# The residual and second bias of a graph network's node update: rows of x added by DVE, in place of a PE product of x's columns

## The chip, the cores and the metric

The kernel runs on one core of one Trainium2 chip. The metric is the device time of one execution in microseconds (us). The engines are named as in the profile: PE multiplies matrices (PEld loads its weights), DVE works on vectors, ACT applies activations, POOL issues the gathers, SP issues plain transfers; ACT issues some too.

## The reference

A graph with 12,500 nodes of 64 features and 200,000 edges sorted by destination. For every edge a two-layer network computes a message; messages are summed per destination; a second two-layer network updates the node, and the node's own row is added and normalised:

```
msg_in     = concatenate([nodes[row], nodes[col], edge_features])   # 64 + 64 + 32
messages   = relu(msg_in @ mW1 + mb1) @ mW2 + mb2                   # 160 -> 128 -> 64
aggregated = segment_sum(messages, col, num_segments=12500)
upd        = relu(concatenate([nodes, aggregated]) @ uW1 + ub1) @ uW2 + ub2
out        = layernorm(x + upd)                                      # over 64 features, no scale
```

## The kernel before

**The first layer by tables.** The products of all nodes with the two node parts of mW1 are made once, as tables in device memory: A (tab_a) for sources and B (tab_b) for destinations, the latter with the bias added. The products need x by columns. In `columns_of` (L396 to L402) all of x's columns are loaded into one large tile, `xall`, by eight transfers at the very start: four on SP's queue for the lower 64 partitions and four on ACT's for the upper. `products` multiplies eight blocks of 128 nodes per call, `chunk_a` (13 chunks) copies one half with ACT and the other with DVE and stores on ACT's queue; `chunk_b` adds the bias on DVE and stores on SP's queue. All of A and the first chunk of B are made before the main loop; the other twelve chunks of B in the loop, from step 8 on.

**Steps.** An edge tile is 128 edges. A step is eight tiles (SUB); there are 196 steps. For step s, POOL gathers the source rows with eight indirect transfers (`gather`, L168). As A is not there at the beginning, the first XG = 7 steps gather rows of x instead (64 features), which PE transposes and multiplies with w1a (`transpose`, and the branch `s < XG` of `node_part`). Two such steps share one of the 14 row buffers; later steps have one buffer each, and `frees(s)` says after which step a buffer can be gathered into again. `windows` issues, on SP, eight transfers of 32 rows of B (L229), since a tile's destinations lie within a window of 32 nodes; `load` and `loadd` (L215, L184) load the edges' features and destinations for two steps at a time, the former after DVE's `select` (L194 to L200) has compared destinations. `edge_part` (L255) multiplies these on PE; `node_part` adds the gathered rows on DVE (L276) and ACT takes the relu (L277); `collect` (L302) sums the hidden rows of a window on PE with a selection matrix, and L307 counts the edges.

**Updates.** The second message layer is folded into the update's weights (`weights`). A period of steps collects up to 448 nodes; there are 34 periods, which start at the steps in `UPD`. At a period's end `close` copies sums and counts, `carry` moves an overlap of 32 nodes on, and `update` (L337, L338) makes the hidden layer. One step later `residual` makes four blocks of 128 nodes: per block one product of x's columns (tile `xw`: row 0 the counts, row 63 ones, below them 64 rows of x) with `ux`, which holds a unit matrix and, in row 63, the second bias (L346), and one of the hidden layer with `u2` (L347). Both accumulate in PSUM tile `py`, which shares two buffers (tag "pc") with the edge products. DVE takes mean and variance from `py` (L351, L353), ACT a square root (L355). A step later `norm` normalises from `py` (L361, L364), and `store` writes on SP's queue (L370). `columns`, two steps ahead of the update, loads `xw` (L330).

**Order.** Every engine's order of work is the program's, written out by hand (`manual_schedule`); waits come from the tiles' uses. In a step of the main loop it is: gathers whose buffers are due, `norm`, `windows(s+2)`, `node_part(s)`, `collect(s-1)`, `close`, then `select`, `load` and `counts` (even steps) or `loadd` (odd), a chunk of B, `edge_part(s+1)`, `carry`, `update`, `residual`, `columns`, the set-up in `rest`, `store`. The pool `work` has two buffers per name.

A general path (`tc.If`, for inputs whose destinations don't fit the windows) does not run with these inputs.

Of the kernel before, what the change touches and what calls it, by code (L numbers as in the profile page):

```python
# [10 lines left out]
F32 = mybir.dt.float32  # L11
I32 = mybir.dt.int32
AF = mybir.ActivationFunctionType
ALU = mybir.AluOpType
# [3 lines left out]
P = 128  # L18
N, D, DE, DH = 12500, 64, 32, 128
E = 200000  # L20
EPS = 1e-5
NB = -(-N // P)
# [12 lines left out]
PADWIN = 1000000  # L35
EK, SK = 0, DE
ROWB = 14
XG = 7
NCH = 8
HB = NCH // 2  # L40
EARLY = NCH * P
# [3 lines left out]
NCOL = (-(-N // P) + UB) * P  # L45
UN = 448
UW = UN + WIN
ONE = D - 1


def updates():
# [12 lines left out]


@with_exitstack
def gnn_kernel(ctx: ExitStack, tc: tile.TileContext, x1T, x, eT, e_rows, src, dst, dst_row, wrow, wnext, whalf,
               mW1, mb1, mW2, mb2, uW1, ub1, uW2, ub2, out):


# [36 lines left out]
    xall = const.tile([P, -(-NB // NCH), HB * P], F32, name="xall")  # L107
    w1b = const.tile([P, DH], F32, name="w1b")
    b1 = const.tile([P, DH], F32, name="b1")

# [12 lines left out]
    ux = const.tile([P, D], F32, name="ux")  # L123
# [49 lines left out]
    with tc.tile_pool(name="sup", bufs=2) as sup, tc.tile_pool(name="work", bufs=2) as work, tc.manual_schedule():  # L173
# [152 lines left out]
        def columns(u):  # L326

            n0 = nc.values_load(usup[0:1, u:u + 1], engines=[ET.SP], min_val=0, max_val=N - 1,
                                skip_runtime_bounds_check_because="destinations are node numbers")
            nc.sync.dma_start(xw[u % 2][ONE:, :UN], x1T[:, bass.ds(n0, UN)])  # L330
            us[u] = n0

        def update(u):

            n0 = us[u]
            pu = psum.tile([DH, UN], F32, name="pu", tag="pc")
            nc.tensor.matmul(pu, w2u, sums_s[u % 2][:, :UN], start=True, stop=False)  # L337
            nc.tensor.matmul(pu, uz, xw[u % 2][:, :UN], start=False, stop=True)  # L338
            nc.scalar.activation(hT[:, :UN], pu, AF.Relu, bias=ub1_s)

        def residual(u):

            n0 = us[u]
            py = psum.tile([P, UB, D], F32, name="py", tag="pc")
            for i in range(UB):
                nc.tensor.matmul(py[:, i], xw[u % 2][:, i * P:(i + 1) * P], ux, start=True, stop=False)  # L346
                nc.tensor.matmul(py[:, i], hT[:, i * P:(i + 1) * P], u2, start=False, stop=True)  # L347
            st = work.tile([P, UB, nc.vector.BN_STATS_DIM], F32, name="st")
            mv = work.tile([P, UB, nc.vector.BN_AGGR_DIM], F32, name="mv")
            for i in range(UB):  # L350
                nc.vector.bn_stats(out=st[:, i], in_=py[:, i])  # L351
            for i in range(UB):
                nc.vector.bn_aggr(out=mv[:, i], in_=st[:, i])  # L353
            sd = work.tile([P, UB], F32, name="sd")
            nc.scalar.activation(sd, mv[:, :, 1], AF.Sqrt, bias=eps)  # L355
            us[u] = (n0, py, mv, sd)

        def norm(u):
            n0, py, mv, sd = us[u]
            rs = work.tile([P, UB], F32, name="rs")  # L360
            nc.vector.reciprocal(rs, sd)  # L361
            o = work.tile([P, UB, D], F32, name="o")
            for i in range(UB):
                nc.vector.tensor_scalar(o[:, i], py[:, i], mv[:, i, 0:1], rs[:, i:i + 1],  # L364
                                        op0=ALU.subtract, op1=ALU.mult)
            us[u] = (n0, o)

# [18 lines left out]


        Av, Bv, B0v = (t.rearrange("(c p) f -> p c f", p=P) for t in (A, B, B0))
        xblocks = x1T[1:, :].rearrange("d (c n) -> d c n", n=P)

        def spread(c):

            n = min(NCH, NB - c)
            return [(h, min(HB, n - HB * h)) for h in range(2) if n > HB * h]

        def columns_of(h, a, b, queue):  # L396

            b = min(b, -(-(NB - HB * h) // NCH))
            if b > a:
                v = xblocks[:, a * NCH + HB * h:, :]  # L400
                queue.dma_start(xall[64 * h:64 * h + 64, a:b].rearrange("d c (i n) -> d c i n", n=P),
                                bass.AP(v.tensor, v.offset, [[v.ap[0][0], D], [NCH * P, b - a], [P, HB], [1, P]]))  # L402

        def products(c, w):
            xl = xall[:, c // NCH]
            pb = psum.tile([P, 2, HB, DH], F32, name="pb", tag="pc")
            for i in range(HB):
                for h, m in spread(c):
                    if i < m:
                        nc.tensor.matmul(pb[:, h, i, :], xl[64 * h:64 * h + 64, i * P:(i + 1) * P],  # L410
                                         w[64 * h:64 * h + 64], start=True, stop=True)
            return pb, work.tile([P, 2, HB, DH], F32, name="tb")

        def chunk_a(c):
            pb, tb = products(c, w1a)
            for h, m in spread(c):
                if h:
                    nc.vector.tensor_copy(tb[:, h, :m], pb[:, h, :m])  # L418
                else:
                    nc.scalar.copy(tb[:, h, :m], pb[:, h, :m])  # L420
            n = min(NCH, NB - c)
            nc.scalar.dma_start(Av[:, c:c + n, :], tb.rearrange("p h i f -> p (h i) f")[:, :n])

        def chunk_b(c, into):
            pb, tb = products(c, w1b)
            n = min(NCH, NB - c)
            pf, tf = (t.rearrange("p h i f -> p (h i) f")[:, :n] for t in (pb, tb))
            nc.vector.tensor_tensor(tf, pf, b1.unsqueeze(1).broadcast_to([P, n, DH]), op=ALU.add)
            for v in into:
                nc.sync.dma_start(v[:, c:c + n, :], tf)  # L430
# [24 lines left out]
        nc.scalar.dma_start(src_s[:, :64], src[:, :64])  # L455
        for h in range(2):
            nc.sync.dma_start(w1a[64 * h:64 * h + D], mW1[0:D, :])
        for a, b in ((0, 1), (1, 3), (3, 7), (7, 13)):
            columns_of(0, a, b, nc.sync)
            columns_of(1, a, b, nc.scalar)  # L460
        nc.scalar.dma_start(src_s[:, 64:], src[:, 64:])
        make_identity(nc, ident)
        nc.gpsimd.iota(slot_i, pattern=[[1, WIN]], base=0, channel_multiplier=0)
# [20 lines left out]
        for k, c in enumerate(range(0, NB, NCH)):  # L484
            chunk_a(c)
            if k == 0:
                chunk_b(0, [B0v, Bv])
            if k == 2:

                w0 = wint[:, :GE * SUP]  # L490
                nc.vector.tensor_scalar(past, w0[:, GE * SUP - 1:], float(EARLY - WIN), None, op0=ALU.is_gt)
                nc.vector.tensor_scalar(w0, w0, float(EARLY - WIN), None, op0=ALU.min)
                windows(0)
                windows(1)
            if k == 4:
                relative(0, 8 * SUP)
            if k == 6:
                offsets()
            if k == 9:
                select(0)  # L500
                load(0)
                counts(0)

        def rest(s):

            if s == 1:
                relative(8 * SUP, 8 * SUP + WCH)
            elif s == 2:
                relative(8 * SUP + WCH, NT)
                halves(4 * SUP, NTP // 2)  # L510
            elif s == BS:
                nc.sync.dma_start(wa, wrow.rearrange("o (p c) -> (o p) c", c=SUP))
                nc.sync.dma_start(wb, wnext.rearrange("o (p c) -> (o p) c", c=SUP))
                nc.scalar.dma_start(w2, mW2)
                nc.scalar.dma_start(u1a, uW1[D:2 * D, :])
                nc.scalar.dma_start(b2c, mb2.rearrange("(f o) -> f o", o=1))
                nc.vector.memset(uz[:D], 0.0)
                nc.vector.memset(ux[:D], 0.0)
                nc.vector.memset(eps, EPS)
# [63 lines left out]
        for s in range(last + 3):  # L583
# [203 lines left out]
```

## Time and profile before

| | |
|---|---|
| median of 3 runs | 2788.36 us (2787.59 to 2792.91) |
| the profiled execution | 2787.59 us, span 2785.8 us, granted PE clock 0.527 |
| busy | PE 1570.8 us (56%), PE weight loads 1374.0 (49%), DVE 536.2 (19%), ACT 341.3 (12%), POOL 1475.7 (53%) |
| transfers | 208.75 MB, mean 75 GB/s |
| gathers (L168) | 56 of x, 1507 of A, 0.94 us each |
| first gather from A, last gather | 134.4 us, 2663.8 us |
| products of residual (L346, L347) | 272 records each, 84.5 and 83.8 us busy |
| x by columns | 8 transfers of 128 to 768 KB |

A row of the profile's groups names the line, the engine, the operation and the tiles (out<-in), then how many there were, how long they were busy, the mean of one and the engine's idle time just before them with what ended most of it. An fp32 product is two matmul records. In the timeline a row is start, length, engine, line, operation and count, with the idle time before it in brackets. "remote" and "issue" mean that no releaser was seen. The chain is followed back from the last instruction to whatever released each one.

### The profile page before, as it was taken

How to read it: one execution, taken by the hardware profiler on the slowest of the kernel's cores; microseconds unless marked ns; L12 is line 12 of the kernel's file. 1: busy time of each engine (PE TensorE's matmuls, PEld its weight loads, DVE VectorE, ACT ScalarE, POOL GpSimd, SP SyncE). 2: the span in 40 equal slices, each digit the busy share in tenths (PEclk: the TensorE clock that was granted, in tenths of full speed). 3: DMA queues.
4: the chain of work that ended last, by engine and by line, in shares of the span. 5: the costliest groups of instructions: out<-in, count | busy, mean ns of one | idle time of the engine just before them, and what ended most of it. 6: DMA issues, size and time to landing. Idle time of an engine off the chain costs nothing.

```text
span 2785.8 us, 34069 instructions
## 1 busy us (share of the span) xinstructions
PE 1570.8 (56%) x9234; PEld 1374.0 (49%) x9234; DVE 536.2 (19%) x1013; ACT 341.3 (12%) x453; POOL 1475.7 (53%) x1572
## 2 busy tenths in 40 slices
PE   1412756564555565645646465555656565576698
PEld 1302645453554455545545454454555455465577
DVE  0300121221211211212212121211122212121232
ACT  0100100110111111111111111111111111111122
POOL 7074545555555565555655555555455555555510
PEclk7555555555555555555555555555555555555565
DMA  5421223333222222222222222222222222222221
GB/s 124 127 74 45 69 77 85 88 86 86 72 72 72 70 78 71 74 66 72 77 67 73 68 75 71 72 69 71 73 71 75 71 73 76 70 77 69 74 73 42
DMA packets 240741, 208.75 MB, mean 75 GB/s; under 512 B 76605, under 2 KB 207167, under 8 KB 240560
## 3 DMA queue, kind: packets, MB, share of 16 engines
q0 software_dynamic: 50016, 100.70, 14.0%
q1 hardware_dynamic: 175998, 96.93, 12.7%
q10 hardware_dynamic: 14546, 8.93, 1.2%
q8 instruction: 87, 1.43, 0.2%
q14 instruction: 94, 0.77, 0.1%
HBM read 188.50 MB, written 17.83 MB: 74 GB/s over the span
## 4 chain that ended last, share of the span: by engine, by line
PE 34%; issue 30%; another core or an unknown queue 16%; SPq 9%; DMA 5%; DVE 4%; ACT 1%; POOL 0%; DVEq 0%; ACTq 0%
PE pc L255 13%; PE sums L302 12%; SPq L229 8%; DMA l<-in_eT 3%; DVE h L276 1%; PE pu L337 1%; PE py L346 1%; PE py L347 1%; PE pu L338 1%; PE cnt L307 1%; PE pb L410 1%; DMA rhs<-tab_b 1%; DMA tab_a<-tb 1%; DVE l L196 1%
## 5 line engine op out<-in xcount | busy, mean ns | idle before, releaser
L168 POOL DMA_INDIRECT xg<-tab_a,src_s x1507 | 1421.7, 943 | 1170.4 <-issue 423.3
L255 PE MATMUL pc<-rhs,l 64*128 64x128 f32 x3126 | 507.5, 430 | 640.5 <-DMA l<-in_eT 317.7
L302 PEld LDWEIGHTS sums<-sel,h 128*128 128x128 f32 x3126 | 664.1, 310 | 331.8 <-issue 327.7
L302 PE MATMUL sums<-sel,h 128*128 128x32 f32 x3126 | 659.0, 372 | 278.9 <-issue 277.3
L255 PEld LDWEIGHTS pc<-rhs,l 64*128 64x128 f32 x3126 | 417.0, 312 | 688.3 <-issue 613.6
L276 DVE TENSOR_TENSOR h<-pc,xg 128x1024 f32<-128x1024 f32 (+1 forms) x190 | 230.2, 1212 | 1009.9 <-issue 466.5
L277 ACT ACTIVATE h<-h 128x1024 f32<-128x1024 f32 (+1 forms) x190 | 199.0, 1048 | 814.6 <-DVE h L276 694.4
L196 DVE TENSOR_TENSOR l<-l,cps 128x1024 f32<-128x1024 int32 (+1 forms) x101 | 123.4, 1221 | 311.0 <-DMA l<-in_dst_row 262.5
L200 DVE TENSOR_TENSOR sel<-cps,drc 128x512 f32<-128x512 f32 x98 | 67.2, 686 | 468.0 <-remote 236.4
L208 ACT CAST selb<-sel 128x512 bf16<-128x512 f32 x98 | 60.4, 616 | 579.4 <-DVE sel L200 277.1
L307 PE MATMUL cnt<-selb,one 128*1 128x32 bf16 x1563 | 83.3, 188 | 42.7 <-issue 40.3
L346 PE MATMUL py<-ux,xw 128*128 128x64 f32 x272 | 84.5, 406 | 12.1 <-issue 12.1
L347 PE MATMUL py<-u,hTu 128*128 128x64 f32 x272 | 83.8, 404 | 8.2 <-issue 7.7
L307 PEld LDWEIGHTS <-one 128*1 128x1 bf16 x1563 | 55.1, 83 | 59.2 <-issue 48.7
L346 PEld LDWEIGHTS py<-ux,xw 128*128 128x128 f32 x272 | 69.7, 311 | 21.2 <-issue 20.5
L347 PEld LDWEIGHTS py<-u,hTu 128*128 128x128 f32 x272 | 71.2, 316 | 10.3 <-issue 9.6
L351 DVE BATCH_NORM_STATS2 st<-py 128x6 f32<-128x64 f32 x136 | 21.3, 219 | 285.9 <-PE py L347 149.3
L410 PE MATMUL pb<-w1a,xall 64*128 64x128 f32 x196 | 25.9, 435 | 86.8 <-DVE tb L418 61.6
L337 PE MATMUL pu<-sums_s,w2u 128*128 128x448 f32 x68 | 63.3, 1023 | 10.3 <-issue 9.8
L410 PEld LDWEIGHTS pb<-w1a,xall 64*128 64x128 f32 x196 | 22.8, 325 | 89.5 <-DVE tb L418 63.7
L168 POOL DMA_INDIRECT xg<-in_x,src_s x56 | 53.0, 946 | 17.9 <-issue 16.8
L338 PE MATMUL pu<-xw,uz 128*128 128x448 f32 x68 | 55.9, 911 | 7.8 <-issue 7.8
(87 smaller groups left out, 443.6 us busy)
## 6 DMA issues: line engine op xcount, KB each, us to landing
l<-in_dst_row SPq DMA_DIRECT2D x196, 128.0 KB
l<-in_eT SPq DMA_DIRECT2D x196, 128.0 KB
rhs<-tab_b SPq DMA_DIRECT2D x1563, 16.0 KB
xg<-tab_a,src_s POOLq DMA_INDIRECT x1507
tab_b<-tb SPq DMA_DIRECT2D x13, 512.0 KB
tab_a<-tb ACTq DMA_DIRECT2D x12, 512.0 KB
out<-o SPq DMA_DIRECT2D x34, 128.0 KB
xw<-in_x1T SPq DMA_DIRECT2D x34, 113.8 KB
```

Of the source, the lines that this page charges most:

```text
L168: nc.gpsimd.indirect_dma_start(out=a[:, i, :] if s < XG else a[:, i // 2, i % 2, :], out_offset=None, in_=A[:, :] if s >= XG else x[:, :], ...
L196: nc.vector.tensor_tensor(l[r], l[r].bitcast(I32), node[r].unsqueeze(2).broadcast_to([r.stop - r.start, SUP // 2, P]), op=ALU.is_equal)
L229: nc.sync.dma_start(r[q:q + WIN, (o + i) // 2, :], tab[bass.ds(ws[i], WIN), :])
L255: nc.tensor.matmul(pc[:, b, k, :], L[g][q:q + 64, m, :], rhs[g % 2][q:q + 64, m, :], start=s >= XG or k == 0, stop=s >= XG)
L276: nc.vector.tensor_tensor(hf[:, m], pf[:, m], a[:, m], op=ALU.add)
L277: nc.scalar.activation(hf[:, m], hf[:, m], AF.Relu)
L302: nc.tensor.matmul(ps[:, bass.ds(ws[i], WIN)], h[:, i % 2, i // 2, :], S[g][:, k0 + i, :], start=False, stop=ends and i == n - 1)
L307: nc.tensor.matmul(pn[:, bass.ds(ws[i], WIN)], one, SB[g][:, k0 + i, :], start=False, stop=ends and i == n - 1)
L337: nc.tensor.matmul(pu, w2u, sums_s[u % 2][:, :UN], start=True, stop=False)
L338: nc.tensor.matmul(pu, uz, xw[u % 2][:, :UN], start=False, stop=True)
L346: nc.tensor.matmul(py[:, i], xw[u % 2][:, i * P:(i + 1) * P], ux, start=True, stop=False)
L347: nc.tensor.matmul(py[:, i], hT[:, i * P:(i + 1) * P], u2, start=False, stop=True)
```

## The change

Three things change together. In the node update the product with `ux` goes; `columns` loads 64 rows into `xw` (x without a row of ones) and, besides, the 512 rows of x of this update into a tile `xr`; `residual` adds `xr` and `py` into a tile `y` on DVE and then the second bias, held in all partitions, and everything after reads `y`. The columns of x for the tables are loaded chunk by chunk into a tile `xl` with two buffers, by up to two transfers each: for A on ACT's queue, two chunks ahead, and for B in the loop on SP's queue, one chunk ahead. And XG is 8, so eight steps gather from x.

```diff
-XG = 7
+XG = 8
...
-            nc.sync.dma_start(xw[u % 2][ONE:, :UN], x1T[:, bass.ds(n0, UN)])
-            us[u] = n0
+            nc.sync.dma_start(xw[u % 2][D:, :UN], xT[:, bass.ds(n0, UN)])
+            xr = work.tile([P, UB, D], F32, name="xr")
+            nc.sync.dma_start(xr, x[bass.ds(n0, UB * P), :].rearrange("(c p) d -> p c d", p=P))
+            us[u] = n0, xr
...
             for i in range(UB):
-                nc.tensor.matmul(py[:, i], xw[u % 2][:, i * P:(i + 1) * P], ux, start=True, stop=False)
-                nc.tensor.matmul(py[:, i], hT[:, i * P:(i + 1) * P], u2, start=False, stop=True)
+                nc.tensor.matmul(py[:, i], hT[:, i * P:(i + 1) * P], u2, start=True, stop=True)
+            y = work.tile([P, UB, D], F32, name="y")
+            nc.vector.tensor_tensor(y, xr, py, op=ALU.add)
+            nc.vector.tensor_tensor(y, y, ub2_b.unsqueeze(1).broadcast_to([P, UB, D]), op=ALU.add)
...
-                nc.vector.bn_stats(out=st[:, i], in_=py[:, i])
+                nc.vector.bn_stats(out=st[:, i], in_=y[:, i])
...
-                nc.vector.tensor_scalar(o[:, i], py[:, i], mv[:, i, 0:1], rs[:, i:i + 1],
+                nc.vector.tensor_scalar(o[:, i], y[:, i], mv[:, i, 0:1], rs[:, i:i + 1],
...
-        def columns_of(h, a, b, queue):
-
-            b = min(b, -(-(NB - HB * h) // NCH))
-            if b > a:
-                v = xblocks[:, a * NCH + HB * h:, :]
-                queue.dma_start(xall[64 * h:64 * h + 64, a:b].rearrange("d c (i n) -> d c i n", n=P),
-                                bass.AP(v.tensor, v.offset, [[v.ap[0][0], D], [NCH * P, b - a], [P, HB], [1, P]]))
+        def columns_of(c, queue):
+
+            xl = work.tile([P, HB * P], F32, name="xl")
+            for h, m in spread(c):
+                o = (c + HB * h) * P
+                queue.dma_start(xl[64 * h:64 * h + 64, :m * P], xT[:, o:o + m * P])
+            xls[c] = xl
...
             n = min(NCH, NB - c)
+            if c + 2 * NCH < NB:
+                columns_of(c + 2 * NCH, nc.scalar)
             nc.scalar.dma_start(Av[:, c:c + n, :], tb.rearrange("p h i f -> p (h i) f")[:, :n])
...
-        for a, b in ((0, 1), (1, 3), (3, 7), (7, 13)):
-            columns_of(0, a, b, nc.sync)
-            columns_of(1, a, b, nc.scalar)
+        columns_of(0, nc.sync)
+        columns_of(NCH, nc.scalar)
...
+        columns_of(NCH, nc.sync)
...
-                nc.vector.memset(ux[:D], 0.0)
...
-                nc.vector.tensor_copy(ux[D:], ident[D:, D:])
...
-                nc.scalar.dma_start(ux[ONE:ONE + 1], ub2.rearrange("(o f) -> o f", o=1))
+                nc.scalar.dma_start(ub2_b, ub2.rearrange("(o f) -> o f", o=1).broadcast_to([P, D]))
...
             if chunks and s >= BS and chunks[0] < NCH + NB * (s + 1 - BS) / (SUP // SUB * (GE - 1) - BS):
+                if len(chunks) > 1:
+                    columns_of(chunks[1], nc.sync)
                 chunk_b(chunks.pop(0), [Bv])
```

More of the change, by code (lines that the diff above doesn't have):

```diff
@@ L47 @@
 UW = UN + WIN
-ONE = D - 1
 def updates():
@@ L66, in gnn_kernel @@
 @with_exitstack
-def gnn_kernel(ctx: ExitStack, tc: tile.TileContext, x1T, x, eT, e_rows, src, dst, dst_row, wrow, wnext, whalf,
+def gnn_kernel(ctx: ExitStack, tc: tile.TileContext, xT, x, eT, e_rows, src, dst, dst_row, wrow, wnext, whalf,
                mW1, mb1, mW2, mb2, uW1, ub1, uW2, ub2, out):
@@ L105, in gnn_kernel @@
     past = const.tile([1, 1], F32, name="past")
-    xall = const.tile([P, -(-NB // NCH), HB * P], F32, name="xall")
     w1b = const.tile([P, DH], F32, name="w1b")
@@ L122, in gnn_kernel @@
     u2 = const.tile([DH, D], F32, name="u2")
-    ux = const.tile([P, D], F32, name="ux")
+    ub2_b = const.tile([P, D], F32, name="ub2_b")
     w2u = const.tile([DH, DH], F32, name="w2u")
@@ L329, in columns @@
                                 skip_runtime_bounds_check_because="destinations are node numbers")
-            nc.sync.dma_start(xw[u % 2][ONE:, :UN], x1T[:, bass.ds(n0, UN)])
-            us[u] = n0
+            nc.sync.dma_start(xw[u % 2][D:, :UN], xT[:, bass.ds(n0, UN)])
+            xr = work.tile([P, UB, D], F32, name="xr")
+            nc.sync.dma_start(xr, x[bass.ds(n0, UB * P), :].rearrange("(c p) d -> p c d", p=P))
+            us[u] = n0, xr
         def update(u):
-            n0 = us[u]
             pu = psum.tile([DH, UN], F32, name="pu", tag="pc")
@@ L341, in residual @@
         def residual(u):
-            n0 = us[u]
+            n0, xr = us[u]
             py = psum.tile([P, UB, D], F32, name="py", tag="pc")
             for i in range(UB):
-                nc.tensor.matmul(py[:, i], xw[u % 2][:, i * P:(i + 1) * P], ux, start=True, stop=False)
-                nc.tensor.matmul(py[:, i], hT[:, i * P:(i + 1) * P], u2, start=False, stop=True)
+                nc.tensor.matmul(py[:, i], hT[:, i * P:(i + 1) * P], u2, start=True, stop=True)
+            y = work.tile([P, UB, D], F32, name="y")
+            nc.vector.tensor_tensor(y, xr, py, op=ALU.add)
+            nc.vector.tensor_tensor(y, y, ub2_b.unsqueeze(1).broadcast_to([P, UB, D]), op=ALU.add)
             st = work.tile([P, UB, nc.vector.BN_STATS_DIM], F32, name="st")
@@ L355, in residual @@
             nc.scalar.activation(sd, mv[:, :, 1], AF.Sqrt, bias=eps)
-            us[u] = (n0, py, mv, sd)
+            us[u] = (n0, y, mv, sd)
         def norm(u):
-            n0, py, mv, sd = us[u]
+            n0, y, mv, sd = us[u]
             rs = work.tile([P, UB], F32, name="rs")
@@ L388, in gnn_kernel @@
         Av, Bv, B0v = (t.rearrange("(c p) f -> p c f", p=P) for t in (A, B, B0))
-        xblocks = x1T[1:, :].rearrange("d (c n) -> d c n", n=P)
+        xls = {}
         def spread(c):
@@ L394, in spread @@
             return [(h, min(HB, n - HB * h)) for h in range(2) if n > HB * h]
-        def columns_of(h, a, b, queue):
-            b = min(b, -(-(NB - HB * h) // NCH))
-            if b > a:
-                v = xblocks[:, a * NCH + HB * h:, :]
-                queue.dma_start(xall[64 * h:64 * h + 64, a:b].rearrange("d c (i n) -> d c i n", n=P),
-                                bass.AP(v.tensor, v.offset, [[v.ap[0][0], D], [NCH * P, b - a], [P, HB], [1, P]]))
+        def columns_of(c, queue):
[4 more added lines that the diff above has]
+            xls[c] = xl
         def products(c, w):
-            xl = xall[:, c // NCH]
+            xl = xls[c]
             pb = psum.tile([P, 2, HB, DH], F32, name="pb", tag="pc")
@@ L751 @@
     x, src, dst, edge = (np.asarray(a) for a in (x, src, dst, edge_attr_32))
-    xp = np.zeros((NPAD, D), x.dtype)
+    xp = np.zeros((NCOL, D), x.dtype)
     xp[:N] = x
-    xc = np.zeros((1 + D, NCOL), x.dtype)
-    xc[0] = 1
-    xc[1:, :N] = x.T
     sp = np.zeros(EPAD, src.dtype)
@@ L766 @@
     arrays = {
-        "x1T": xc, "x": xp,
+        "xT": xp.T, "x": xp,
         "eT": ep.reshape(NSUP, SUP // 2, 2, P, DE).transpose(0, 2, 4, 1, 3), "e_rows": ep,
```

## The prediction

> **What bounds the kernel now.** I read the chain that ended last first, then what each engine waited for, then the three stages in which those waits lie. The chain, by engine and by line:
>
> ```profile
> PE 34%; issue 30%; another core or an unknown queue 16%; SPq 9%; DMA 5%; DVE 4%; ACT 1%; POOL 0%; DVEq 0%; ACTq 0%
> PE pc L255 13%; PE sums L302 12%; SPq L229 8%; DMA l<-in_eT 3%; DVE h L276 1%; PE pu L337 1%; PE py L346 1%; PE py L347 1%; PE pu L338 1%; PE cnt L307 1%; PE pb L410 1%; DMA rhs<-tab_b 1%; DMA tab_a<-tb 1%; DVE l L196 1%
> ```
>
> PE's own work is a third, and "issue", in which nothing shown is awaited, is nearly another third. POOL has no share although it is never far from full: its 1563 gathers come every 1.25 us (943 ns and a gap of 0.30). The table of waits shows the loop that this makes:
>
> ```profile
> POOL xg L168 <- DVE h L276: 341.1, 60, 18.6
> PE pc L255 <- DMA l<-in_eT: 317.7, 47, 19.1
> PE pc L255 <- issue: 286.5, 203, 17.8
> PE pc L255 <- DVE o L364: 21.0, 13, 5.0
> ```
>
> (microseconds, times, longest.) POOL waits for the addition in h to free a buffer; PE waits for operands that SP loads. Why SP is late is in the timeline, SP beside a gather burst and without one:
>
> ```profile
> 1119.51 20.46 SPq L229 DMA_DIRECT2D rhs<-tab_b  x8
> 1140.67 0.02 SPq L215 DMA_DIRECT2D l<-in_eT  x2
> 1141.82 2.69 PE L255 MATMUL pc<-rhs,l 64*128 64x128 f32 x16 [18.02 <-DMA l<-in_eT]
> ...
> 2692.02 4.19 SPq L229 DMA_DIRECT2D rhs<-tab_b  x8
> ```
>
> Eight transfers cost 20.5 us under gathers and 4.2 without: 2.56 against 0.52 each. PE is slowed in the same stretches; at 171 to 205 it starts one matmul each 2.8 us. So a gather burst stops the rest, the rest catches up while POOL waits, and what the rest must do then is on the path. The same at the start, before table A is complete (ACT and PE):
>
> ```profile
> 42.16 2.08 PE L410 MATMUL pb<-w1a,xall 64*128 64x128 f32 x16 [16.38 <-issue]
> 80.11 0.58 ACT L420 COPY tb<-pb 128x512 f32<-128x512 f32 x1 [70.60 <-remote]
> ```
>
> The 56 gathers of x run from 2.9 to 72.7 us; ACT's second chunk of A comes at 80.1, though its products had run at 24. From 80.1 to 134.4 the other chunks follow and POOL idles.
>
> The sum stands against the profiled execution: span 2785.8, with what lies around it 2787.6 us, 0.8 below the median of 2788.4.
>
> **The change part by part.**
>
> *Residual products (L346) go.* They are 272 of 9234 matmul records:
>
> ```profile
> L346 PE MATMUL py<-ux,xw 128*128 128x64 f32 x272 | 84.5, 406 | 12.1 <-issue 12.1
> L330 SPq DMA_DIRECT2D xw<-in_x1T x34: 3/367/710, 693.2 to 2752.1; - x34
> ```
>
> Busy 84.5 us is the most, nothing the least, if PE then only waits longer. The chain by lines gives L346 1.4% of 2785.8: 39 us on the path. PE goes from this block to the sums without a wait, so I take **-39**.
>
> *py's PSUM buffer is freed earlier.* It was held through statistics, square root and normalisation, until L364; now until the first addition. PE waited 21.0 us for L364. Between -21 and 0; what follows (the addition in h) still stands behind the normalisation on DVE, so I take half: **-10**.
>
> *Two DVE additions of 128x256 per update, 68 in all.* From 686 ns at 512 elements (L200) and 1221 at 1024 (L196) a line gives 0.42 us at 256: 28 us. They stand ahead of the statistics, the normalisation and the next addition in h, for which ACT and POOL wait; but PE ends the block some 1.8 us sooner (eight passes at 0.21), which covers 0.84. Without that cover the 28 are paid. Statistics and normalisation now read SBUF: at best L364's 335 ns falls to the 190 of the SBUF copy in L521, 136 x 0.145 = 20 us gained. Between -20 and +28, nearer to the covered case: **+6**.
>
> On POOL, gathers show 938/944/967 ns (min, median, max), so no DVE instruction now holds one up, and L364 reads PSUM now. The Trainium skill, SBUF — State Buffer, "Who interferes with whom", speaks against the change here: a tensor_scalar with its operands in SBUF can take the mode with two ports and then shuts GpSimd out for the whole instruction. By that rule the 136 instructions of L364 could each hold up a gather by their 0.335, 46 us at most, and the sum would be 2811; no row here shows it, and the sum goes by the row, zero.
>
> *SP's queue.* 34 loads of rows of x (128 KB; also an address computation and a move) and 21 loads of columns for B's chunks in the loop. They stand ahead of the next step's eight windows, behind which stand the operand loads that PE waits for 317.7 us. L330, the nearest load, takes 0.37 and some 0.07 around it; the store of B 0.42. That is 34 x 0.44 + 21 x 0.42 = 24 us in clear stretches, 55 x 2.56 = 141 under bursts; at least 55 x 0.145 = 8 (chain: SPq L229 8.1%, 226 us over 1563). SP's work under a burst is done anyway before POOL's wait ends, so an addition mostly pushes one clear transfer behind it: between 8 and 24, **+16**.
>
> *The start.* (a) XG 8 instead of 7: 64 gathers of x instead of 56, 8 x 1.25 = +10 before POOL is quiet. One step more goes through transposes: the activations of steps 3 to 7 stand at 274.5 to 308.6, +7. One step less is paced by gathers: from 258 to 2500 us POOL makes 1323 of them, 1.69 us each, eight of them -14. (b) In each of eleven chunks of A, ACT issues up to two column loads ahead of the store. Issue (2 x 0.37) lies beside DVE's half of the copy (0.69); the transfer, 256 KB at the 290 GB/s that the DMA view shows in the busiest slices, 0.9, ahead of a store that the next copy awaits. With some 0.2 of issue, 1.1 over nine chunks: +10; nothing if another of the 16 DMA engines' stretches hides it, +20 with half of a store's 3.2 each. (c) 3.2 MB no longer stand ahead of the first bias and the weights of B, whose products ran at 21.7; they may run near 8, before the burst tells, and one to four more chunks of A (4.6 us apart at 81 to 97) get done early: -5 to -18, I take two, -9; nothing if the burst tells sooner. Sum of the start **+4**, between -25 and +40. Behind ACT's first column load, which waits for the first B products, stands the first store of A.
>
> Smaller: SP waits for the last A products before it reloads the columns of chunk 8, with step 2's windows behind it; these are due only after the burst from 134 to 243, which hides some 10 us. Two memsets' worth of setup changes: nothing.
>
> Sum: -39 - 10 + 6 + 16 + 4 = -23; 2787.6 - 23 = 2764.6, **2765 us**.
>
> **The rivals.**
>
> *SP pays the burst's price (slower).* For it: 20.46 us for eight windows and PE's 317.7 us behind SP. Against: bursts end by their own buffers. The other terms sum to -39, so it decides from 0.71 us per added transfer; half of 2.56, 1.28, gives 70: 2819 us.
>
> *POOL paces, PE's relief buys nothing (slower).* For it: in that long middle 1.25 of each 1.69 us is POOL's. Against: POOL waits 341 us for the addition in h, which waits for PE. Zero in place of -49 gives +26: 2814 us.
>
> *PE's relief counts in full.* The block's L346 part measured from start to start is 69.5 us; with the buffer's 21, DVE's +6, SP's 8 and a start at -15: -91, 2697; I put this case near 2710, as not every block can lie on the path.
>
> *It cancels.* Half the gain on PE (-25), the rest as taken: +1, within 0.2%, 2789.
>
> **How the numbers follow.** Forecast 0.36 (own range 2745 to 2780), full relief 0.08, cancelling 0.10, SP 0.25, POOL 0.21. A time within 0.2% (5.6 us) can't be told from no change. Faster 0.44, same 0.10, slower 0.46: the single likeliest case is a gain, while the two that lose hold as much together. The range reaches from 2722 (most of the full relief left out) to 2832, over both slower cases but not SP's price paid whole (141: 2892).
>
> **What would show it.** Right: L346 gone and L347's chain share no larger; PE's wait for L364 near zero; SP's transfers for x and xr at 0.4 to 0.5 in clear stretches; PE's wait for in_eT within 20 us of 317.7; first gather from A between 125 and 150 (134.4 now). Wrong: that first gather beyond 160; PE's wait for in_eT, or for SP at all, up by 50; gathers longer than 967 ns; POOL's waits unchanged while PE idles more.

## The result, and the profile after

The change makes the kernel slower by 0.8%: 2803.61 us (median of 20 runs, 2793.85 to 2823.05) against 2783.57 us (20 runs of the kernel before beside them, 2767.02 to 2796.95), a ratio of 1.0076 with a 95% interval of 1.0057 to 1.0096, so about 20 us. The forecast was 2765 us. The two profiled executions are 2793.85 us (span 2792.0) after and 2787.59 us before, only 6 us apart, because after's is the fastest of its 20 runs and before's one of the slower of its own. Their traces can show where work and waits moved, not the whole 20 us, and runs of one kernel lie up to 30 us apart.

The operations came out as taken. These are the groups of the node update in the kernel after (line, engine, operation, tiles, count | busy us, mean ns of one | idle time before):

```profile
L344 PE MATMUL py<-u,hTu 128*128 128x64 f32 x272 | 62.0, 402 | 1.1 <-ACT hTu L337 0.7 <-issue 0.4
...
L364 DVE TENSOR_SCALAR o<-y,mv,rs 128x64 f32<-128x64 f32 x136 | 33.4, 310 | 1.2
...
L347 DVE TENSOR_TENSOR y<-y,ub_b 128x256 f32<-128x256 f32 x34 | 14.4, 425 | 1.2
L346 DVE TENSOR_TENSOR y<-xr,py 128x256 f32<-128x256 f32 x34 | 14.3, 421 | 250.2 <-remote 92.3 <-PE py L344 85.6 <-PE sums L299 41.3
```

The product with `ux` is gone, each DVE addition takes 0.42 us, and the normalisation costs 0.31 us in place of 0.335. What PE got for it is in the busy line of the page:

```profile
PE 1550.0 (56%) x8982; PEld 1344.5 (48%) x8982; DVE 557.5 (20%) x1078; ACT 342.0 (12%) x454; POOL 1476.6 (53%) x1572
```

PE is busy 20.8 us less than before (1570.8) although 272 records went: the records of the edge products alone (L252, L255 before) took 21.3 us more. DVE is busy 21.3 us more. The waits tell what became of PE's free time (engine and line that waited, what for, us in total, times, longest). Two of before first, then after:

```profile
POOL xg L168 <- DVE cps L194: 310.7, 55, 16.2
...
PE pc L255 <- DMA rhs<-tab_b: 7.2, 10, 1.8
```

```profile
POOL xg L165 <- DVE cps L191: 351.0, 63, 15.2
...
PE pc L252 <- DMA l<-in_eT: 334.1, 59, 20.3
...
POOL xg L165 <- DVE h L273: 312.1, 56, 14.4
...
PE pc L252 <- issue: 246.6, 158, 19.7
...
PE pc L252 <- DMA rhs<-tab_b: 63.9, 30, 16.0
```

Both operands that PE waits for here are loaded by SP. The wait for the edges' features rose from 317.7 to 334.1 us and the one for windows of B from 7.2 to 63.9: 73 us more together. But "issue" ahead of the same products fell from 286.5 to 246.6, and both traces hold under half of the landing records of SP's transfers (14,324 of 33,008 and 15,078 of 33,888), so part of the 73 may have changed its name only. The groups of these products, before and after, give all idle time ahead of them:

```profile
L255 PE MATMUL pc<-rhs,l 64*128 64x128 f32 x3126 | 507.5, 430 | 640.5 <-DMA l<-in_eT 317.7
L252 PE MATMUL pc<-rhs,l 64*128 64x128 f32 x3126 | 528.8, 436 | 664.9 <-DMA l<-in_eT 334.1
```

It rose by 24 us, about as much as PE's busy time fell. The waits behind the normalisation, 21.0 us of PE's idle time before, are 3.8 now. POOL's waits for DVE (additions in h, and `cps`) are 663 us, 652 before: POOL was not released earlier. The timeline of SP shows the added loads in their places, after, and then a load of `xw` in the kernel before:

```profile
1122.87 17.94 SPq L226 DMA_DIRECT2D rhs<-tab_b  x8
1142.21 1.40 SPq L212 DMA_DIRECT2D l<-in_eT  x2
1144.39 0.53 SPq L327 DMA_DIRECT2D xw<-in_xT  x1
1145.12 0.43 SPq L329 DMA_DIRECT2D xr<-in_x  x1
1146.38 5.36 SPq L226 DMA_DIRECT2D rhs<-tab_b  x8
...
2694.46 0.53 SPq L327 DMA_DIRECT2D xw<-in_xT  x1
2695.19 0.42 SPq L329 DMA_DIRECT2D xr<-in_x  x1
2696.45 4.58 SPq L226 DMA_DIRECT2D rhs<-tab_b  x8
```

```profile
1141.20 0.36 SPq L330 DMA_DIRECT2D xw<-in_x1T  x1
1142.63 3.13 SPq L229 DMA_DIRECT2D rhs<-tab_b  x4
```

Eight windows still take up to 17.9 us while POOL gathers, and 4.6 to 5.4 in the other rows shown. What the reader should measure here is not the length of the row load (0.43) but how much later the next step's windows start, counted from the start of `xw`: 1.99 us in both places shown, 1.43 before. Over all updates the medians are 2.21 and 1.58, so a row load pushes the windows back by some 0.6 us. The address computation and the register move are in it.

At the start, the second copy of A still comes late, and the first gather from A is at 138.9 us (134.4 before). The timeline of ACT:

```profile
14.70 0.58 ACT L420 COPY tb<-pb 128x512 f32<-128x512 f32 x1 [10.39 <-remote]
42.05 1.12 ACTq L401 DMA_DIRECT2D xl<-in_xT  x2
43.27 0.54 ACTq L424 DMA_DIRECT2D tab_a<-tb  x1
86.94 0.58 ACT L420 COPY tb<-pb 128x512 f32<-128x512 f32 x1 [71.66 <-remote]
```

The first store of A (17.6 us before) stands behind a column load that is issued at 42 us only.

The two traces agree with a late loss: the sums of step 60 start 3 us earlier than before (1014.5 us, 1017.5), those of step 190 9 us later (2741.1, 2732.2), and the column loads of the loop end at 653 us. For one pair of runs this is a hint and no more.

The chain that ended last can't be set beside that of before: it accounts for under 30% of the span, where before it reached 99%.

```profile
PE 11%; issue 8%; SPq 2%; another core or an unknown queue 2%; DVE 2%; DMA 1%; POOL 1%; ACT 0%; DVEq 0%; ACTq 0%; POOLq 0%
```

### The profile page after: what moved, and what is told of

It is laid out like the page before. It is cut to its first block, busy times and chain, and to the rows that moved or that the text cites. A ratio compares the mean times of both kernels' runs of the same rounds, so it can differ in the third digit from the quotient of the medians.

```text
span 2792.0 us, 33797 instructions
## 1 busy us (share of the span) xinstructions
PE 1550.0 (56%) x8982; PEld 1344.5 (48%) x8982; DVE 557.5 (20%) x1078; ACT 342.0 (12%) x454; POOL 1476.6 (53%) x1572
## 5 line engine op out<-in xcount | busy, mean ns | idle before, releaser
L252 PE MATMUL pc<-rhs,l 64*128 64x128 f32 x3126 | 528.8, 436 | 664.9 <-DMA l<-in_eT 334.1
L252 PEld LDWEIGHTS pc<-rhs,l 64*128 64x128 f32 x3126 | 433.8, 313 | 725.3 <-issue 654.5
L273 DVE TENSOR_TENSOR h<-pc,xg 128x1024 f32<-128x1024 f32 x189 | 228.9, 1212 | 1101.7 <-issue 623.0
L274 ACT ACTIVATE h<-h 128x1024 f32<-128x1024 f32 x189 | 198.0, 1048 | 809.9 <-DVE h L273 721.5
L410 PE MATMUL pb<-w1a,xl 64*128 64x128 f32 x196 | 31.0, 441 | 99.3 <-DMA xl<-in_xT 62.8
L410 PEld LDWEIGHTS pb<-w1a,xl 64*128 64x128 f32 x196 | 26.4, 323 | 103.6 <-issue 88.8
L346 DVE TENSOR_TENSOR y<-xr,py 128x256 f32<-128x256 f32 x34 | 14.3, 421 | 250.2 <-remote 92.3
L337 ACT ACTIVATE hTu<-pu,ub_s 128x448 f32<-128x448 f32 x34 | 21.5, 633 | 347.1 <-PE pu L336 155.5
L344 PE MATMUL py<-u,hTu 128*128 128x64 f32 x272 | 62.0, 402 | 1.1 <-ACT hTu L337 0.7
L344 PEld LDWEIGHTS py<-u,hTu 128*128 128x128 f32 x272 | 55.8, 303 | 9.3 <-issue 6.5
L410 PE MATMUL pb<-w1b,xl 64*128 64x128 f32 x196 | 34.4, 440 | 14.2 <-issue 14.0
```

Source lines behind the costliest of these rows:

```text
L252: nc.tensor.matmul(pc[:, b, k, :], L[g][q:q + 64, m, :], rhs[g % 2][q:q + 64, m, :], start=s >= XG or k == 0, stop=s >= XG)
L273: nc.vector.tensor_tensor(hf[:, m], pf[:, m], a[:, m], op=ALU.add)
L274: nc.scalar.activation(hf[:, m], hf[:, m], AF.Relu)
```

## The experiments

**The same kernel under another condition.** All the following comparisons ran on six chips on each of which the kernel before takes 1992 to 1995 us, not 2784. Which chip the first comparison ran on is not on record, so "the first chip" stands here for that chip in the state that it had then; whether the chip or its state made the difference is not shown. The timeline of the residual part alone (first run below) shows what differs, SP first and then POOL in the same stretch:

```profile
1008.19 0.79 SPq L215 DMA_DIRECT2D l<-in_eT  x2
1009.82 4.90 SPq L229 DMA_DIRECT2D rhs<-tab_b  x8
```

```profile
1000.30 0.94 POOL L168 DMA_INDIRECT xg<-tab_a,src_s  x1 [0.30 <-issue]
1001.55 0.94 POOL L168 DMA_INDIRECT xg<-tab_a,src_s  x1 [0.30 <-issue]
```

The gathers are the same, one per 1.25 us, but eight windows beside them take 4.9 us, not 20. POOL gathers without a pause from the first gather from A to the last and paces everything: the other engines wait for it. Five runs were made in this condition; each was timed beside the kernel before.

*The residual part alone* (columns and XG as before):

```diff
-            nc.sync.dma_start(xw[u % 2][ONE:, :UN], x1T[:, bass.ds(n0, UN)])
+            nc.sync.dma_start(xw[u % 2][D:, :UN], x1T[1:, bass.ds(n0, UN)])
+            nc.sync.dma_start(xr, x[bass.ds(n0, UB * P), :].rearrange("(c p) d -> p c d", p=P))
...
-                nc.tensor.matmul(py[:, i], xw[u % 2][:, i * P:(i + 1) * P], ux, start=True, stop=False)
...
+            nc.vector.tensor_tensor(y, xr, py, op=ALU.add)
+            nc.vector.tensor_tensor(y, y, ub2_b.unsqueeze(1).broadcast_to([P, UB, D]), op=ALU.add)
```

> The residual part alone: rows of x loaded by SP per update and added on DVE, no unit-matrix product; columns by eight transfers and XG 7 as before. If SP's queue carries the loss (34 loads more, at about 1.3 us each on the path, PE's 49 us of relief bought only in part): slower by 5 to 25 us. If the loss lies at the start (columns, XG): this part alone is faster by 15 to 40 us, as the prediction's terms -39, -10, +6 and +10 say. If PE's relief buys nothing and SP's loads cost their clear 0.44 us: slower by 5 to 20 us.

Measured: 1994.86 against 1994.65 us, ratio 1.0004 (0.9995 to 1.0012): nothing.

*The columns' part alone*:

```diff
-        for a, b in ((0, 1), (1, 3), (3, 7), (7, 13)):
-            columns_of(0, a, b, nc.sync)
-            columns_of(1, a, b, nc.scalar)
+        columns_of(0, nc.sync)
+        columns_of(NCH, nc.scalar)
...
+                columns_of(chunks[1], nc.sync)
```

> The columns part alone: x's columns chunk by chunk, on ACT's queue for A and on SP's for B, in place of eight transfers. If SP's queue carries the loss: slower by 10 to 30 us, with the first gather from A where it was. If the start does: slower by 5 to 20 us, and the first gather from A later than 134.4 by as much. If both are hidden: within 5 us.

Measured: 1985.8 us, ratio 0.9961 (0.9948 to 0.9974), 9 us gained.

*The eighth x step alone*:

```diff
-XG = 7
+XG = 8
```

> XG 8 in place of 7 alone. The prediction's terms are +10 for the longer burst, +7 for one more transposed step, -14 for one step less that gathers pace: within 5 us. If the burst at the start is passed on whole and nothing comes back: slower by 10 to 17 us, the first gather from A at 144 to 147.

Measured: 1984.66 us, ratio 0.9951 (0.9939 to 0.9963), 10 us gained. The expectations of these three runs were written for the condition of the first comparison; none of them foresaw its result.

*The products taken away, nothing in their place* (residual and second bias left out):

```diff
-                nc.tensor.matmul(py[:, i], xw[u % 2][:, i * P:(i + 1) * P], ux, start=True, stop=False)
-                nc.tensor.matmul(py[:, i], hT[:, i * P:(i + 1) * P], u2, start=False, stop=True)
+                nc.tensor.matmul(py[:, i], hT[:, i * P:(i + 1) * P], u2, start=True, stop=True)
```

> The kernel before without the product of x's columns with the unit matrix (L346): the residual and the second bias are left out, nothing stands in their place, loads as before. It measures PE's relief by itself. If it lies on the path as the chain says: faster by 30 to 45 us. If gather bursts pace the kernel: within 10 us of before.

Measured: 1993.0 us, ratio 0.9988 (0.9980 to 0.9997), 2 us gained.

*The whole change once more*:

> The whole change again, beside the kernel before on the same chip. In the four runs of the parts the kernel before took 1995 us, not 2784: gathers ran back to back from 83 us to the end, PE and SP were not slowed beside them, and POOL paced everything. If the chip is like that one: the parts add up, 0 (residual), -9 (columns) and -10 (XG) give -19, so about 1976 us. If the chip is like the one of the first comparison, where bursts of gathers stop PE and SP: 20 us slower than before, at 2790 to 2810 us. The claim that PE's relief and SP's added transfers don't matter where POOL paces needs the first; the loss of the first comparison then belongs to the slowing beside the gathers alone.

Measured: 1980.80 against 1992.51 us, ratio 0.9941 (0.9928 to 0.9955): 12 us **faster**; the sum of the parts, 19, was expected for such a chip. So the sign of the change depends on what paces. Where POOL paces, only POOL's idle time before A is complete can be won. Two of POOL's waits, without the products and then with the whole change:

```profile
POOL xg L168 <- issue: 469.0, 1538, 0.3
POOL xg L168 <- DMA tab_a<-tb: 12.5, 1, 12.5
```

```profile
POOL xg L165 <- issue: 466.1, 1529, 0.3
POOL xg L165 <- DMA xg<-tab_a,src_s: 8.5, 28, 0.3
```

There are 12.5 us of it. The columns and the eighth x step win most of it each for itself, which is why 9 and 10 add up to 12 and not to 19. In the whole change the wait for A is gone. Row loads, PE's relief (the work that was taken from it) and DVE's additions lie beside the gathers: together they come to nothing, the relief alone to 2 us.

**Taking POOL out of the way.** To see what the rest costs where POOL does not pace, half of the gathers from A were left out (four in each step from step 21 on, 22 in the changed kernel), and each gathered row was added to two edges' products, so that DVE's addition keeps its size:

```diff
+            if XG + ROWB <= s < NSUB - 1 and i % 2:
+                continue
             nc.gpsimd.indirect_dma_start(
...
+                if XG + ROWB <= s < NSUB - 1:
+                    half = a[:, :SUB // 2].unsqueeze(1).broadcast_to([P, 2, SUB // 2, DH])
+                    nc.vector.tensor_tensor(h, pc, half, op=ALU.add)
```

A second pair also loads SP, with one unread load of 16 KB behind each window's:

```diff
+                if s >= XG + ROWB:
+                    nc.sync.dma_start(scr[i], mW1[:WIN, :])
```

> The kernel before with half of its gathers from A (four a step in place of eight from step 21 on, each row added to two edges' products; half of the source rows is left out of the result, DVE's addition keeps its size). At 1.249 us a gather POOL then needs about 867 x 1.25 + 83 = 1167 us, and PE, busy for 1386 us in the run of the residual alone, should pace: 1450 to 1700 us in place of 1994. It is the ground for the next run. If POOL's gathers pace in another way than by their number, the time stays above 1800.

> The changed kernel with the same half of its gathers (half of the source rows left out). Theory 1 (what the prediction took): where PE paces, the 272 products that the change removes are worth 30 to 62 us (272 x 0.228 us at most), so it ends 30 to 62 us below the kernel before with half of its gathers, and some 10 us more if the start counts too. Theory 2 (PE's relief buys nothing even where PE has most to do, because its steps wait for windows from SP or for h): within 10 us of it. Theory 3 (SP's 55 transfers pace): 14 to 25 us above it.

> The kernel before with half of its gathers and, from step 21 on, one more load of 16 KB on SP behind each window's load, into tiles that nothing reads (half of the source rows left out). 1400 transfers more at 0.43 to 0.59 us are 600 to 820 us of SP's time. If SP then paces, the time rises above the kernel with half of the gathers alone by 200 us and more; if SP has that much room, by less than 50.

> The changed kernel with half of its gathers and the same added loads on SP (half of the source rows left out). Where SP paces, theory 3 (SP pays for each of the change's 34 row loads and 21 column loads, and PE's relief is worth nothing there) expects 14 to 25 us (55 x 0.26 to 0.45 us) above the kernel before with the same loads; theory 1 (PE's relief counts everywhere) expects 20 us or more below it; within 8 us either way tells that SP's loads lie in its idle time even then.

Measured with half of the gathers: 1444.10 us before, 1459.60 after, 15.5 us slower. With the loads on SP besides: 2088.93 and 2115.13, 26.2 slower. (The medians of these runs are uncertain by 2 to 4 us, a difference by some 5; that of the eighth x step below by 8.) A loss of the size of the first comparison's is back, on chips on which the full kernel gains; PE, busy for 56% there, has 88 to 90% to do here, so it need not be the same loss. The added loads cost 645 us for 1395, 0.46 each, so that SP paces there. The busy lines of before and after, half of the gathers:

```profile
PE 1299.6 (90%) x9234; PEld 1156.1 (80%) x9234; DVE 535.3 (37%) x1013; ACT 340.0 (24%) x453; POOL 819.9 (57%) x876
```

```profile
PE 1280.3 (88%) x8982; PEld 1127.4 (77%) x8982; DVE 555.9 (38%) x1078; ACT 340.5 (23%) x454; POOL 824.2 (57%) x880
```

Then the parts, each against 1444.10 us, or 2088.93 with the loads on SP. The products alone (the edit of the fourth run):

> The kernel before with half of its gathers (half of the source rows left out) and without L346, the 272 products of x's columns with the unit matrix (residual and second bias left out), nothing else changed; PE is busy for 90% of the span in the kernel with half of the gathers. The ground is that kernel, 1444 us. If PE's relief is worth what PE is busy with those products (64.0 us there): 1380 to 1415. If it is worth nothing, because each step waits for what SP brings: within 6 us of 1444.

> The kernel before with half of its gathers, the added loads on SP, and no L346 (half of the source rows, residual and second bias left out). If SP paces and PE's relief is then worth nothing: within 6 us of 2089 us. If the relief is worth what it was without the added loads: 8 to 14 us below. If it is worth what PE is busy with those products: 60 to 79 us below.

Measured: 1432.93 us, 11 gained; with the loads on SP 2087.69, 1 gained, which is none. The second is the clearest reading of the study. PE's waits without and then with the products taken away, and PE's busy time in the latter:

```profile
PE pc L260 <- DMA l<-in_eT: 414.5, 74, 8.9
PE pc L260 <- issue: 79.6, 16, 8.3
```

```profile
PE pc L260 <- DMA l<-in_eT: 472.8, 76, 8.9
PE pc L260 <- issue: 104.9, 16, 8.6
```

```profile
PE 1408.7 (67%) x8962; PEld 1236.8 (59%) x8962; DVE 528.5 (25%) x1013; ACT 339.4 (16%) x453; POOL 819.6 (39%) x876
```

PE is busy 80 us less (1489.2 with the products) and waits 84 us more, 58 of them for what SP brings. The time does not move. (PE's busy time is no exact measure: the run with the row loads below has the same products as 1489.2 and shows 1466.0.) Even at 90% PE, without the loads, PE's busy time falls by 22 us (to 1277.9) and the time by 11; PE's wait for in_eT takes most of the rest (29.6 to 39.0).

Row loads alone, unread, on SP:

```diff
             nc.sync.dma_start(xw[u % 2][ONE:, :UN], x1T[:, bass.ds(n0, UN)])
+            xr = work.tile([P, UB, D], F32, name="xr")
+            nc.sync.dma_start(xr, x[bass.ds(n0, UB * P), :].rearrange("(c p) d -> p c d", p=P))
```

> The kernel before with half of its gathers (half of the source rows left out), and beside each load of columns on SP the changed kernel's load of 512 rows of x, which nothing reads: 34 SP transfers more, nothing else. If SP's queue pays for each: 34 x 0.43 to 0.60 us, 14 to 20 us above 1444. If the cost lies in DVE's additions or in the column loads: within 4 us of 1444.

> The kernel before with half of its gathers, the added 16 KB loads on SP, and 34 unread row loads on SP (half of the source rows left out). The ground is the same kernel without the row loads, 2089 us. If SP paces and each load costs what an added one does there ((2089 - 1444) / 1396 = 0.46 us): 16 us above it. If a load of 512 rows costs more than one of 16 KB: up to 26 us above it. If SP has room: within 6 us of it.

Measured: 1456.73 us, 13 lost (0.37 each); with the loads on SP 2112.21, 23 lost (0.68 each), nearly all of the 26 that the whole change loses there. These are SP's instructions for it where SP paces:

```profile
L342 SPq MOVE xr<-in_x x34: 29/29/29, 385.8 to 2080.7; - x34
L342 SPq DMA_DIRECT2D xr<-in_x x34: 398/403/409, 385.8 to 2080.8; - x34
```

The transfer instruction is 0.40 us, the distance from the load of `xw` to it 0.57 (median), the price 0.68. From `xw` to the next windows it is 2.00 in place of 1.44 (medians).

The residual part alone, the columns alone, the eighth x step alone:

> The residual's part of the change alone, with half of the gathers (half of the source rows left out): row loads, two additions on DVE an update, no product with the unit matrix; columns as before. If SP alone pays: the same as with the unread row loads, 14 to 20 us above 1444. If DVE's additions cost too: 28 us (66 x 0.423) more. If PE's relief counts: below 1444.

> The columns' part of the change alone (a load of 32 or 64 columns' blocks for each chunk in place of eight at the start), with half of the gathers (half of the source rows left out). The ground is the kernel before with half of its gathers, 1444 us. If SP pays for the 21 column loads there: 4 to 12 us above it, and steps 20 to 40 take about 141 us in place of 130. If the rest of the loss comes from elsewhere: within 3 us of it, or below it by the 9 us that it gained at the start with all gathers.

> The kernel before with the eighth x step alone (XG = 8) and half of its gathers (half of the source rows left out). With all gathers it gained 10 us of POOL's idle time at the start. If POOL's idle time at the start counts without POOL pacing later: 5 to 10 us below 1444. If only PE's work counts (16 more products with x's rows, four transposes and a copy, no wait saved): 0 to 4 us above it.

Measured: 1451.99 us for the residual part, 8 lost. Rows (+12.6) and relief (-11.2) leave some 6.5 for DVE's additions; no run has these alone. The waits show how they cost, before and after with half of the gathers:

```profile
PE sums L309 <- ACT h L280: 11.2, 13, 1.1
PE sums L306 <- ACT h L277: 50.5, 25, 2.9
```

PE's sums wait for ACT's relu, which comes after DVE's addition in h. Every run with the two new additions and half of the gathers alone shows 43 to 51 us of this wait (44.9 for the residual part alone), every one without them 6 to 11. So part of PE's relief goes into a wait behind DVE, not behind SP. The columns alone: 1459.01, 15 lost, more than expected. The eighth x step: 1443.24, no difference. The parts add up to 22, the whole is 15.5; the sum holds within its uncertainty only. Steps 20 to 40, by DVE's additions in h, take 142 us with the columns' part, 130 before, as expected; by the starts of the edge products they take 142.1 and 139.1, so how much is lost there depends on what is counted. The products taken away (11 gained), the residual part (8 lost) and the eighth step (no difference, 5 to 10 gained or up to 4 lost expected, with a spread of 17 us) fit no branch of their expectations well: each lies between them.

Last, the loads moved to ACT's queue, rows first, then the column loads of the later chunks too:

```diff
-            n0 = nc.values_load(usup[0:1, u:u + 1], engines=[ET.SP], min_val=0, max_val=N - 1,
+            n0 = nc.values_load(usup[0:1, u:u + 1], engines=[ET.SP, ET.Activation], min_val=0, max_val=N - 1,
...
-            nc.sync.dma_start(xr, x[bass.ds(n0, UB * P), :].rearrange("(c p) d -> p c d", p=P))
+            nc.scalar.dma_start(xr, x[bass.ds(n0, UB * P), :].rearrange("(c p) d -> p c d", p=P))
...
-                    columns_of(chunks[1], nc.sync)
+                    columns_of(chunks[1], nc.scalar)
```

> The changed kernel with half of its gathers (half of the source rows left out), its 34 row loads issued on ACT's queue in place of SP's. The ground is the changed kernel with half of its gathers, 1460 us. If SP's queue pays for the row loads: 10 to 20 us below that. If the transfers themselves or DVE's additions cost: within 4 us of it.

> The changed kernel with half of its gathers (half of the source rows left out), its 34 row loads and the column loads of the later chunks issued on ACT's queue in place of SP's. The ground is the same with only the row loads moved, 1448.5 us; the kernel before with half of its gathers had 1444. If the columns' part costs SP's queue: 5 to 14 us below 1448.5, at or below the kernel before, and steps 20 to 40 near 131 us. If it costs through its two buffers or its transfers: within 4 us of 1448.5 and steps 20 to 40 near 142 us.

Measured: 1448.51 us with the rows on ACT, 11 below the changed kernel; 1442.04 with the columns too, another 6 (the intervals of these two overlap). That is the time of the kernel before with half of its gathers (ratios to the full kernel before 0.7242, 0.7227 to 0.7257, and 0.7249, 0.7237 to 0.7261). So most of this loss is in SP's queue, not in the transfers: on ACT's queue the same loads cost no more than PE's relief gives. One sign of the last expectation failed: steps 20 to 40 still take 142 us with the column loads on ACT, so that stretch is not SP's; what makes it long was not found. With all gathers, or on the first chip, these two versions were not run.

## Why the prediction was wrong

**What bounds the kernel: half right.** That gathers stop the rest and that the rest catches up is what that chip's traces show, before and after. What the forecast read into it, that PE's work in the catching up is on the path, the result and the runs speak against. (POOL, "never far from full" in the prediction, is busy for 53% of that span.)

**Residual products, -39, and py's buffer, -10: the step that failed.** "The chain by lines gives L346 1.4% ... PE goes from this block to the sums without a wait, so I take -39." A share of a chain says where the chain passed, not what the time would be without that work: after the block PE comes to the next operands from SP, and where these are no earlier it waits for them. Taken away alone, the products are worth 11 us where PE has 90% to do, 1 where SP paces, 2 where POOL paces. In the pair of the first comparison the normalisation's wait went, as said (21.0 to 3.8 us), and PE was busy 20.8 us less, but the idle time ahead of the edge products, whose operands SP loads, grew by 24 us all the same.

**SP's queue, +16: sign right, size open.** A row load was priced at 0.44 by the length of the nearest load; it pushes the next windows back by 0.6 in the kernel after. The 34 row loads alone, 15 us by that price, cost 13 us (0.37 each) where PE has 90% to do and 23 (0.68) where SP paces.

**DVE, +6: not contradicted.** The sum of the parts leaves 6.5, uncertain by as much; each addition is 0.42 us, as estimated. The rule of the Trainium skill weighed in the prediction (SBUF — State Buffer, "Who interferes with whom") had no occasion to show on the first chip: there no normalisation runs beside a gather, before or after (0 of 136 in both traces), so the prediction's row of 938 to 967 ns said nothing of it either. In the residual part alone 128 of the 136 do, reading SBUF, and this is the row of the gathers there:

```profile
L168 POOL DMA_INDIRECT xg<-tab_a,src_s x1507: 940/945/1141, 83.7 to 1967.1; - x189
```

The 64 gathers beside them have a median of 947 ns and none is longer than 1002; a normalisation takes 310 ns there in the median and up to 467, against at most 345 in the fourth run, which normalises from PSUM: if anything is held up, it is DVE, and by less than 0.2 us. A gather that waited for a whole normalisation, as by the rule, would be near 1250; none is.

**The start, +4: not contradicted.** The first gather from A moved by 4.5 us, within the 125 to 150 given, and at step 60 the kernel after is not behind. Its terms do not carry to other chips, where columns and the eighth x step gain 9 and 10.

**The rivals.** The time is nearest to that of "PE's relief buys nothing" (2814), which gave zero in place of -49. Its reason, that POOL paces, holds in the later runs with all gathers, where the relief is worth 2 us and yet the change gains 12 at the start. On the first chip POOL waits 652 us for DVE, and it is SP behind which the relief seems to be lost. "SP pays the burst's price" was decided from 0.71 us a load only as long as the relief was believed; without it, the plain price of a load is enough. Of the signs given for an error three came: PE's waits that are named for SP, up by 73 (with the doubt above), two gathers longer than 967 ns, and POOL's waits unchanged while PE idles 27 us more. But the signs for being right came too (PE's wait for in_eT 16.4 above 317.7, its wait for L364 near zero, the first gather from A at 138.9; the chain's share of the products can't be compared), so those could not tell a gain from a loss. Two sums are slightly off and decide nothing: eight passes at 0.21 are 1.7 us, not 1.8, and SP's price paid whole gives 2890, not 2892.

**What stays open.** No later run met the condition in which gathers slow the rest, so the parts were not taken apart under the condition of the first comparison. That SP's loads and PE's worthless relief make up its 20 us is argued from the waits of its two traces and from the runs in which SP or PE paces; it is not shown on that chip. A delay behind DVE's additions, as in the runs with half of the gathers, is the rival that stays (PE's sums wait 8.7 us for ACT's relu in the trace after, 0.7 before).

## What to carry to other kernels

Before work is moved from one engine to another, ask for each what it waits for next: time freed on an engine that then waits for a queue was worth 1 us here, and a load added to that queue cost 0.68 us, more than its transfer instruction (0.40) and than the distance by which it moved its neighbours (0.57). A share of the chain is not a saving (39 us by the share; 11, 2 and 1 us in the runs); ask what the engine waits for right behind the removed work. And a load that can go on the queue of an engine with time to spare (ACT, busy 12% of the full kernel) need not go on the one that feeds PE: with half of the gathers the move gave 11 us.

## What was not expected of the hardware

The same kernel takes 2784 us in the first comparison and 1992 to 1995 on the six chips of the later runs. POOL's gathers are alike (944 and 945 ns, one per 1.25 us); what differs is what other engines' instructions cost beside them: eight windows on SP 18 to 20 us on the first, 4.9 on another. What makes the difference no run shows. The traces of the first also hold few records of landed gathers (some 3,400 to 3,600 of the 25,008 that 1,563 gathers would leave, 16 each, against some 23,900 in the run of the residual alone), so that "issue" and "remote" in their waits partly stand for transfers that were not seen. That alone does not break a chain: the one before reaches 99% with so few, and that of the residual alone accounts for about 1%.
